# The last image of a convolution and attention kernel: x and the first two outputs summed in chunks during the last block, two rows completed by VectorE, two pairs in another buffer

## The chip, the cores and the metric

The kernel runs on one core of a Trainium2 chip. The metric is the device time of one execution in microseconds (us); lower is better. The profile is of one such execution; its times are counted from the start of its span, the stretch from the first to the last instruction.

## What is computed

x has 16 images of 128 channels and 64 x 64 points. Layer 0 normalizes each group of four channels of an image, rounds the result to 8 bits, adds a cubic term and convolves it 3 x 3 with three weight sets. The three outputs are each rounded and clipped, and summed with weights; the sum is scaled, biased and added to x. Layer 1 normalizes again, projects to q, k and v of 64 channels, mixes exp(k) and exp(k) v by exp(B), and adds the projected result.

```python
outs = [jnp.einsum('bctfyx,ocyx->btfo', fv, g[i]) for i in range(WP - 1)]
mem_out = adc(outs[-1])
for i, bit in enumerate(reversed(range(WP - 1))):
    mem_out = mem_out + adc(outs[i]) * 2.0 ** bit
mem_out = mem_out * output_factor
# layer 1, after  x = x + layer0(gn(x)):
num = jnp.einsum('ji,bit->bjt', eB, ek * v)
den = jnp.einsum('ji,bit->bjt', eB, ek)
out = q * (num / den)
out = jnp.einsum('oj,bjt->bot', Wm, out)
```

## The kernel before

The convolution is done in a transformed form (Winograd in both directions). Four rows of outputs come from six transformed row sets ("points"). A block is the work on one image and one weight set, so there are 48 blocks, in two halves each: half 0 with points 1 and 2, half 1 with points 3 and 4. Points 0 and 5 join at the end.

The program is one long list of named operations. A name such as `q31.5` is an operation, and the number after a plus sign says how many turns back its image lies. A turn holds the three blocks of one image, the input work of the next image and the second layer of the one or two before. The order of the list is the order in which each engine issues; an operation that has to wait holds up all that follow it on its engine. `ORDER` gives the steady turns, `FIRST` the first, and `LAST` the last: the rest of turn 14, turn 15 with the last image, and turn 16 with what is left. In `LAST`, +2 belongs to turn 14, +1 to turn 15, +0 to turn 16. The last image is image 15.

Names that matter, with k = 0 to 5 for the half that is being worked on:

- TensorE: `q1`, `q2`, `q0`, `q3` are the matmuls of a half with the points u = 0 and 1, into `pa` and `pb` (L556). `P.k` is the matmul that even and odd columns of an outer row share (`shared`), `o0.k` and `o1.k` the two outer matmuls of each column (`outer`), all into `py`. `kp`, `vp`, `qp` (L749) are projections of a pair, `dn` (L759) the mixing, `op` (L771) the output projection.
- ScalarE: `m1`, `sd`, `sA` copy `pa` (L579, L581, L584). `tk.k` (`take`, L633) reads the finished outer row from `py` as int16. `xn` (L796) normalizes the input of a pair, `ek`, `g`, `ln`, `ex`, `r` (L800, L775, L805, L806, L782) are steps of a pair. `cx` (`chunk`, L699) scales the summed outputs of a quarter of an image, `sq` and `ts` (L364) sum squares.
- VectorE: `Bo`, `df`, `sm` (L587, L588, L594) combine the points, `ma` and `mc` (`middle`, L610) make the two middle rows, `S0` and `S3` (`total`, L615 and L618) the sums that outer rows need, `bc` (`spread`, L625) adds these to the shared column in PSUM and spreads it over both columns, `bA`, `bB` (L636) clip, and `ekv`, `u`, `oa`, `ob`, `oc` (L801, L804, L807 to L809) are steps of a pair.
- GpSimd (POOL) issues transfers that add to their target: `sm.k` for even k (L596), `aA`, `aB` of the second and third weight set into `acc` (L643), `cdx` (x onto the scaled sum, L702) and `rd` (residual of a pair, L812). SP issues the plain ones: `li`, `lj` (loads of x), `st` (stores of a pair, L813).

An image is 4 pairs of 1024 points of each channel (`Pair`). In the steady turns a pair's normalized input, its result and the source of its store are one of two buffers, `xns[:, p % 2]`, so pair 2 of an image waits for the store of pair 0 of the same image, and pair 3 for that of pair 1.

The third block of image 15 is finished differently (`Last`, `End`, `LastPair`). Its names begin with t: `tma`, `tmc` make the middle rows, `tS0`, `tS1` the sums, `tP0`, `tP1` the shared matmuls, `tbc`, `tbd` the `spread`s, `tp0`, `tp1`, `to0`, `to1` the outer matmuls (the half h = 1 in `pb`, h = 0 in `py`), `tk0` and `tk3` the `take`s of rows 0 and 3, `tb0` to `tb3` the clipping. `ta0` to `ta3` add each clipped row to `acc` on VectorE (L684). Meanwhile SP has loaded x of image 15 into `x2e`, a view of `gmat`, in four chunks (`Lx0` to `Lx3`, L717). `tx0` to `tx3` (`part`, L724) then compute x + ofs * acc for a row and sum it, `ts0` to `ts3` sum its squares. After these come the norm (`tna` to `tnd`), and four pairs named with capitals (`Xn`, `Kp`, ...), each with buffers of its own.

Of the kernel before, what the change touches and what calls it, by code (L numbers as in the profile page):

```python
# [94 lines left out]
START = "x0 xa pmx xb pvx xc xl xd gr0 er0 cp gr1 er1 pb1 pa1 cs1 cq1 cd1"  # L95

LAST = """
    cl0+2 sA1.2+2 S3.2+2 q31.2+2 lj3+2 st2+2 q10.3+2 cl1+2 P.2+2 bc.2+2 m10.3+2 q11.3+2 m11.3+2
    s0+2 q20.3+2 q21.3+2 o0.2+2 Bo.2+2 va0+2 s1+2 va1+2 sd0.3+2 o1.2+2 bA.2+2 sd1.3+2 q01.3+2
    sq1+2 sq2+2 lj2+2 gr0+2 sq3+2 q30.3+2 q00.3+2 tk.2+2 sA1.3+2 er0+2 q31.3+2 sA0.3+2 ya+2  # L100
    df.2+2 n3+2 n2+2 pmy+2 yb+2 P.3+2 bc.3+2 Bo.3+2 cp+2 q11.4+2 pvy+2 q10.4+2 yc+2 cl3+2
    df.3+2 o0.3+2 m10.4+2 m11.4+2 o1.3+2 q20.4+2 q21.4+2 yl+2 s3+2 yd+2 xn0+2 sd0.4+2 sd1.4+2
    kp0+2 vp0+2 sm.3+2 tk.3+2 P.4+2 q01.4+2 cl2+2 sm.2+2 ek0+2 va3+2 mc.4+2 s2+2 st3+2 aA.2+2
    S0.4+2 ekv0+2 bc.4+2 dn0+2 sA1.4+2 g0+2 q00.4+2 sA0.4+2 va2+2 u0+2 xn1+2 ln0+2 o1.4+2 gr1+2
    o0.4+2 q30.4+2 oa0+2 ex0+2 kp1+2 er1+2 tk.4+2 qp0+2 ob0+2 vp1+2 q11.5+2 ma.4+2 oc0+2 S3.4+2
    ek1+2 m11.5+2 pb0+2 op0+2 r0+2 ekv1+2 q31.4+2 Bo.4+2 rd0+2 q10.5+2 pa0+2 m10.5+2 st0+2
# [12 lines left out]
    sm.1+1 q10.3+1 mc.2+1 S0.2+1 q31.2+1 cd3x+1 bc.2+1 e5+1 o0.2+1 ma.2+1 sq1+1 o1.2+1 S3.2+1
    sA1.2+1 Lx0+0 m10.3+1 tk.2+1 Bo.2+1 bA.2+1 q11.3+1 m11.3+1 q20.3+1 P.3+1 df.2+1 q21.3+1  # L120
    sd0.3+1 q00.3+1 bc.3+1 Lx1+0 o1.3+1 sq2+1 sd1.3+1 q30.3+1 st3+1 sq3+1 sA0.3+1 st2+1 ya+1
    pmy+1 yb+1 q31.3+1 pvy+1 yc+1 yl+1 Bo.3+1 q01.3+1 sA1.3+1 yd+1 sm.2+1 df.3+1 sm.3+1 q10.4+1
    m10.4+1 mc.4+1 o0.3+1 xn0+1 S0.4+1 q11.4+1 tk.3+1 kp0+1 vp0+1 P.4+1 ek0+1 ekv0+1 q20.4+1
    bc.4+1 xn1+1 dn0+1 g0+1 u0+1 sd0.4+1 o0.4+1 m11.4+1 oa0+1 ln0+1 o1.4+1 ex0+1 q21.4+1 ob0+1
    tk.4+1 kp1+1 ma.4+1 qp0+1 vp1+1 aA.2+1 oc0+1 S3.4+1 ek1+1 op0+1 ekv1+1 sd1.4+1 r0+1 q00.4+1
    q01.4+1 sA1.4+1 P.5+1 rd0+1 dn1+1 g1+1 bc.5+1 q11.5+1 bA.4+1 o1.5+1 st0+1 o0.5+1 sA0.4+1
    q30.4+1 u1+1 q10.5+1 aA.4+1 ln1+1 tk.5+1 oa1+1 ex1+1 xn2+0 qp1+1 ob1+1 q31.4+1 oc1+1 bB.3+1
    Bo.4+1 op1+1 kp2+0 r1+1 m10.5+1 vp2+0 aB.3+1 q20.5+1 df.4+1 ek2+0 m11.5+1 ekv2+0 sd0.5+1
    q21.5+1 sd1.5+1 dn2+0 q30.5+1 q01.5+1 g2+0 u2+0 ln2+0 oa2+0 rd1+1 q31.5+1 sA1.5+1 st1+1
    q00.5+1 qp2+0 bB.5+1 ex2+0 aB.5+1 Bo.5+1 xn3+0 sA0.5+1 kp3+0 vp3+0 ob2+0 oc2+0 op2+0 ek3+0  # L130
# [13 lines left out]
def conv_preact_kernel(  # L144
# [29 lines left out]
    P = 128  # L174
# [247 lines left out]
    class Input:  # L422
# [5 lines left out]
        def load(self, q):  # L428
            sp.dma_start(self.x[q], rows(x, self.b, q))
# [125 lines left out]
    def mm(o, w, r, start, stop):  # L555
        pe.matmul(  # L556
            o if len(r.shape) == 2 else o.rearrange("p (t w) -> p t w", w=W2), w, r,
            start=start, stop=stop, skip_group_check=True,
        )


    class Block:
# [35 lines left out]
        def part(self, h):  # L598

            a = acc[:, 1:3] if h == 0 else acc[:, 0:4:3]  # L600
            return (a if self.i == 0 else ys[h]), a
# [63 lines left out]
    class Last(Block):  # L665


        def value(self, r):
            return ys[r in (0, 3)][:, r // 2]

        def operations(self):
            o = {
                "tma": lambda: self.middle(0), "tmc": lambda: self.middle(1),
            }
            for h, z in ((0, py), (1, pb)):
                o |= {
                    f"tS{h}": lambda h=h: self.total(h), f"tP{h}": lambda h=h, z=z: self.shared(h, z),
                    f"tb{'cd'[h]}": lambda h=h, z=z: self.spread(h, z), f"tk{3 * h}": lambda h=h, z=z: self.take(h, z),
                }
                for c in range(2):  # L680
                    o[f"t{'op'[h]}{c}"] = lambda h=h, c=c, z=z: self.outer(h, c, z)
            for r in range(4):
                o[f"tb{r}"] = lambda r=r: self.bound(self.value(r))
                o[f"ta{r}"] = lambda r=r: dve.tensor_tensor(acc[:, r], acc[:, r], self.value(r), ALU.add)  # L684
            return o

    class End:
# [25 lines left out]
            return o  # L713


        def load(self, q):
            sp.dma_start(self.x2[q], rows(x, self.b, q))  # L717

        def row(self, r):
            return x2e.rearrange("p q (t r w) -> p r (q t) w", r=4, w=W)[:, r]  # L720

        def part(self, r, k):
            t = self.row(r)
            dve.scalar_tensor_tensor(  # L724
                t, acc[:, r], ofs, t, ALU.mult, ALU.add, accum_out=self.sums[:, 0, k : k + 1]
            )

        def part_square(self, r, k):
# [139 lines left out]
    def operations(c):  # L868

        o = {}  # L870
        for k in range(6):
            i, h = divmod(k, 2)
            if c < B:
                o |= blocks[c, i].half(h, k)
            if 0 < c < B or (c == 0 and i):
                o |= blocks[(c, i - 1) if i else (c - 1, 2)].rest(k)
        if c < B:
            o["p0"] = lambda: inputs[c].point(0, v[:, 0])
            o["e0"] = lambda: inputs[c].pairs(0)
            o["e5"] = lambda: inputs[c].pairs(1)  # L880
            o["p5"] = lambda: inputs[c].point(5, v[:, 1])
        if 0 < c < B:
            ends[c - 1] = End(c - 1, inputs[c - 1].norm.mean, x2s)
            o |= ends[c - 1].operations()
            for p in (0, 1):
                o |= Pair(ends[c - 1], p).operations()
        if 1 < c:
            for p in (2, 3):
                o |= Pair(ends[c - 2], p).operations()
        if c + 1 < B:  # L890
            inputs[c + 1] = Input(c + 1)
            o |= inputs[c + 1].operations()
        return o
# [64 lines left out]
```

## Time and profile before

| | us |
|---|---|
| three runs | 1597.41, 1597.85, 1602.0; median 1597.85 |
| profiled execution, its own time | 1598.49 |
| its span | 1596.8 |
| busy: TensorE, VectorE, ScalarE, GpSimd | 1487.7, 1479.8, 1183.0, 224.0 |
| mean granted TensorE clock | 0.981 |
| last outer matmul of the convolution ends | 1553.99 |
| last `part` (tx3) ends | 1559.05 |

A steady turn takes about 94 us. Busy times count the engine's own instructions; a wait belongs to the engine that stands still. A line with "<-" after a time names what ended an engine's wait. Records of a matmul with 512 columns come in twos.

### The profile page before, as it was taken

The page shows a single profiled execution, that of the slowest core. Times are in us where ns is not written, and L with a number is a line of the kernel's source. Part 1 is how long each engine was busy: PE and PEld are TensorE (multiplying, and loading weights), DVE is VectorE, ACT ScalarE, POOL GpSimd, SP SyncE. Part 2 cuts the span into 40 slices and gives each one's busy share as a digit, 9 for nine tenths or more (in the row PEclk, how much of TensorE's full clock was granted, in tenths as well). Part 3 has the DMA queues.
Part 4 walks back from the last instruction along what each step waited for, and adds up shares of the span by engine and source line. Part 5 has one row for each costly group of instructions (what it writes and reads, how often), then busy time and mean ns, then how long its engine had stood idle before and what let it go on. Part 6 is the DMA issues. An engine that isn't in the chain of part 4 may idle for free.

```text
span 1596.8 us, 14936 instructions
## 1 busy us (share of the span) xinstructions
PE 1487.7 (93%) x4680; PEld 563.4 (35%) x4680; DVE 1479.8 (93%) x1919; ACT 1183.0 (74%) x1857; POOL 224.0 (14%) x250
## 2 busy tenths in 40 slices
PE   1798999999999999999999999999999999999985
PEld 0233433333333333333333343333333333333321
DVE  7999999999999999999999999999999999998775
ACT  7656878787777878778787877878778787766655
POOL 2001011121201112020111201111120111202010
PEclk6899999999999999999999999999999999999998
DMA  6235467594746758465684746659474675836462
GB/s 186 79 92 120 103 160 171 126 204 114 148 128 164 184 119 196 120 137 141 150 205 109 156 131 150 166 132 203 117 152 132 156 176 121 196 66 119 119 158 80
DMA packets 67361, 227.03 MB, mean 142 GB/s; under 512 B 7632, under 2 KB 8272, under 8 KB 67280
## 3 DMA queue, kind: packets, MB, share of 16 engines
q0 software_dynamic: 37904, 123.42, 42.1%
q1 hardware_dynamic: 29088, 101.59, 17.9%
q10 hardware_dynamic: 288, 1.05, 0.2%
q8 instruction: 37, 0.61, 0.2%
q14 instruction: 44, 0.36, 0.1%
HBM read 102.30 MB, written 33.55 MB: 85 GB/s over the span
## 4 chain that ended last, share of the span: by engine, by line
PE 58%; DMA 14%; issue 11%; DVE 11%; ACT 5%; POOL 2%; DVEq 0%; POOLq 0%; ACTq 0%; SPq 0%
PE py L556 19%; PE pa L556 18%; DMA x<-in_x_dram 5%; PE pz L749 5%; PE pb L556 5%; PE pz L759 3%; PE py L749 3%; DMA s<-s 3%; DMA acc<-y 3%; PE py L771 3%; ACT x L699 2%; DVE acc L610 1%; ACT gs L364 1%; DVE y L610 1%; DVE s L615 1%
## 5 line engine op out<-in xcount | busy, mean ns | idle before, releaser
L556 PE MATMUL py<-v,ud 128*128 128x512 f32 x760 | 357.0, 608 | 1.9 <-DVE py L625 1.3
L556 PE MATMUL pa<-cs,us 128*128 128x512 f32 x384 | 199.1, 620 | 41.7 <-DVE cs L514 31.9
L556 PE MATMUL pa<-cd,us 128*128 128x512 f32 x384 | 203.9, 622 | 11.7 <-ACT pb L581 11.7
L556 PE MATMUL pa<-cq,us 128*128 128x512 f32 x384 | 198.1, 612 | 11.3 <-ACT d L579 11.2
L556 PEld LDWEIGHTS py<-v,ud 128*128 128x128 f32 x760 | 138.9, 189 | 184.0 <-issue 148.9
L556 PE MATMUL pb<-cd,us 128*128 128x512 f32 x384 | 194.5, 602 | 1.9 <-ACT pb L581 1.7
L579 ACT ACTIVATE d<-pa 128x512 f32<-128x512 f32 x192 | 112.2, 594 | 37.8 <-PE pa L556 28.0
L812 POOL DMA_DIRECT2D xn<-x x60 | 59.9, 998 | 567.8 <-ACT xn L782 567.5
L581 ACT ACTIVATE pb<-pa 128x512 f32<-128x512 f32 x192 | 112.5, 586 | 31.3 <-PE pa L556 30.7
L584 ACT ACTIVATE s<-pa 128x512 f32<-128x512 f32 x192 | 110.4, 591 | 32.0 <-PE pa L556 29.9
L749 PE MATMUL pz<-xn,w 128*64 128x512 f32 x480 | 121.8, 607 | 1.3 <-ACT xn L796 1.2
L587 DVE SCALAR_TENSOR_TENSOR s<-d,pb 128x1024 f32<-128x1024 f32 x96 | 117.2, 1221 | 3.6 <-PE pb L556 3.2
L643 POOL DMA_DIRECT2D acc<-y x62 | 68.5, 1105 | 360.8 <-DVE y L636 212.2
L588 DVE TENSOR_TENSOR d<-s 128x1024 f32<-128x1024 f32 x96 | 117.5, 1224 | 1.6 <-ACT s L584 1.5
L633 ACT ACTIVATE y<-py 128x1024 int16<-128x1024 f32 x63 | 84.0, 1334 | 46.0 <-PE py L556 44.8
L782 ACT ACTIVATE xn<-py,scalars 128x512 f32<-128x512 f32 x120 | 76.0, 685 | 56.1 <-PE py L771 56.0
L556 PEld LDWEIGHTS pa<-cs,us 128*128 128x128 f32 x384 | 66.3, 191 | 139.6 <-issue 67.0
L556 PEld LDWEIGHTS pa<-cq,us 128*128 128x128 f32 x384 | 68.0, 190 | 119.5 <-issue 69.4
L556 PEld LDWEIGHTS pa<-cd,us 128*128 128x128 f32 x384 | 66.4, 190 | 123.6 <-ACT pb L581 56.9
L556 PEld LDWEIGHTS pb<-cd,us 128*128 128x128 f32 x384 | 70.2, 190 | 96.0 <-issue 85.2
L556 PE MATMUL py<-sv,ud 128*128 128x512 f32 x190 | 97.7, 596 | 3.3 <-ACT y L633 3.2
L596 POOL DMA_DIRECT2D s<-s x48 | 45.9, 956 | 339.5 <-DVE d L588 127.9
(224 smaller groups left out, 2651.8 us busy)
## 6 DMA issues: line engine op xcount, KB each, us to landing
xc<-in_x_dram SPq DMA_DIRECT2D x121, 512.0 KB, 5.6
acc<-y POOLq DMA_DIRECT2D x62, 512.0 KB, 5.5
x<-in_x_dram POOLq DMA_DIRECT2D x60, 512.0 KB, 10.4
xn<-x POOLq DMA_DIRECT2D x60, 512.0 KB, 4.9
out_dram<-xn SPq DMA_DIRECT2D x60, 512.0 KB, 5.1
s<-s POOLq DMA_DIRECT2D x48, 512.0 KB, 6.3
gmat<-in_x_dram SPq DMA_DIRECT2D x5, 512.0 KB, 8.9
x<-in_g_neg_dram SPq DMA_DIRECT2D x2, 576.0 KB, 11.4
```

The source lines that it names most:

```text
L556: pe.matmul(o if len(r.shape) == 2 else o.rearrange("p (t w) -> p t w", w=W2), w, r, start=start, stop=stop, skip_group_check=True,)
L579: f"m1{u}.{k}": lambda u=u, a=a: act.activation(d[:, u], a, AF.Copy),
L581: f"sd{u}.{k}": lambda a=a, b=b: act.activation(b, a, AF.Copy, scale=-1.0),
L584: f"sA{u}.{k}": lambda u=u, a=a: act.activation(s[:, u, 0], a, AF.Copy),
L587: f"Bo.{k}": lambda: dve.scalar_tensor_tensor(s[:, :, 1], d, 2.0, pb, ALU.mult, ALU.add),
L588: f"df.{k}": lambda: dve.tensor_tensor(d, s[:, 1], s[:, 0], ALU.subtract),
L633: act.activation(self.column(self.part(1)[0], h), y, AF.Copy)
L643: pool.dma_start(a, y, accum_op=ALU.add)
L749: pe.matmul(self.tiles(o)[h * IC : (h + 1) * IC], w, x[:, t[0] : t[1] : t[2]], start=True, stop=True)
L759: pe.matmul(o[c, t], eb[r, c], self.half(x)[r, t], start=True, stop=True, skip_group_check=True)
L782: act.activation(g[:, t], self.tiles(self.op[h]), AF.Identity, bias=bias_sb)
L812: "rd": lambda: pool.dma_start(self.r, self.x2, accum_op=ALU.add),
```

## The change

In the third block of image 15:

- The sum of the first two weight sets' outputs, which is complete in `acc` once `aA.4+1` and `aB.5+1` have landed, is scaled into `x2e` by ScalarE in four chunks (`Lc0` to `Lc3`, `early`). x is then added by four accumulating transfers of POOL (`Lx0` to `Lx3`, `input`) instead of being loaded by SP. `part` adds ofs times the clipped row of the third weight set to that; `ta0` to `ta3` are dropped.
- `shared` is issued for both columns, so the two `spread`s (`tbc`, `tbd`) are dropped. `tk0` and `tk3` are now `complete` on VectorE: PSUM plus the sum of the other points, as int16. The half h = 1 goes to `pz` instead of `pb`.
- In turn 16, pairs 2 and 3 of image 14 have their normalized input, result and source of the store in `f` instead of `xns`.
- `LAST` is written anew throughout. `rd0+1`, `rd1+1`, `st0+1`, `st1+1` (the residuals and stores of pairs 0 and 1 of image 14) now stand after the norm of image 15; `Lx0` and `Lx1` stand in turn 16's part instead of turn 15's; `tk.5+2`, `ln1+2`, `ex1+2` precede `xn2+1`, and `sA1.1+1` precedes `cx0+1`.

```diff
@@ LAST, the part from the end of the last image's convolution to its norm
-    q00.5+1 qp2+0 bB.5+1 ex2+0 aB.5+1 Bo.5+1 xn3+0 sA0.5+1 kp3+0 vp3+0 ob2+0 oc2+0 op2+0 ek3+0
-    r2+0 df.5+1 tma+0 ekv3+0 sm.5+1 tS1+0 dn3+0 g3+0 u3+0 ln3+0 tP1+0 tbd+0 ex3+0 qp3+0 sm.4+1
-    oa3+0 ob3+0 oc3+0 tp0+0 op3+0 tmc+0 tS0+0 tb2+0 tp1+0 Lx2+0 Lx3+0 r3+0 tP0+0 tb1+0 ta1+0
-    tbc+0 to1+0 tx1+0 ta2+0 tk3+0 tx2+0 tb3+0 tsh+0 to0+0 ta3+0 tk0+0 tb0+0 ts1+0 ta0+0 ts2+0
-    tx0+0 ts0+0 tx3+0 ts3+0 tna+0 tpm+0 rd2+0 tnb+0 tpv+0 tnc+0 tnl+0 tnd+0 Xn0+0 Xn2+0 Xn1+0
+    g1+1 u1+1 ln1+1 o0.5+1 q30.4+1 oa1+1 tk.5+1 ex1+1 m10.5+1 bB.5+1 xn3+0 aB.5+1 kp2+0 qp1+1
+    ob1+1 oc1+1 sA1.4+1 vp2+0 op1+1 ek2+0 ekv2+0 q11.5+1 r1+1 dn2+0 g2+0 oa2+0 m11.5+1 u2+0
+    Lc0+0 Lx0+0 q20.5+1 ln2+0 ex2+0 q31.4+1 Bo.4+1 sd0.5+1 q21.5+1 ob2+0 kp3+0 qp2+0 oc2+0
+    vp3+0 Lc1+0 op2+0 sd1.5+1 q01.5+1 ek3+0 ekv3+0 dn3+0 df.4+1 q30.5+1 Lc2+0 sA1.5+1 g3+0
+    q31.5+1 Lx2+0 q00.5+1 r2+0 u3+0 ln3+0 oa3+0 Bo.5+1 ex3+0 ob3+0 qp3+0 sA0.5+1 df.5+1 sm.4+1
+    tP1+0 tp0+0 Lx1+0 oc3+0 sm.5+1 tma+0 op3+0 Lc3+0 Lx3+0 r3+0 tmc+0 tb1+0 tp1+0 tP0+0 tS1+0
+    tb2+0 tS0+0 rd3+0 tx1+0 tk3+0 tsh+0 ts1+0 to0+0 tx2+0 ts2+0 to1+0 tk0+0 tb3+0 tb0+0 tx0+0
+    ts0+0 tx3+0 ts3+0 st3+0 tna+0 tpm+0 tnb+0 tpv+0 tnc+0 tnl+0 tnd+0 Xn0+0 Xn2+0 Xn1+0 Kp0+0
+    rd1+1 Vp0+0 Ek0+0 rd0+1 Eq0+0 Kp1+0 Dn0+0 Ek1+0 Gg0+0 Uu0+0 Xn3+0 st1+1 Vp1+0 Oa0+0 Kp2+0
...
-        def shared(self, h, y):
-            mm(y[:, 1], ud[self.i][:, h, 0], sv[:, h], True, True)
+        def shared(self, h, y, c=1):
+            mm(y[:, c], ud[self.i][:, h, 0], sv[:, h], True, True)
...
+        def complete(self, h, y):
+            t = self.d[0] if h else ss[1][:, 1]
+            dve.tensor_tensor(self.column(self.part(1)[0], h), y, t, ALU.add)
+
         def value(self, r):
             return ys[r in (0, 3)][:, r // 2]
...
-            for h, z in ((0, py), (1, pb)):
+
+            for h, z in ((0, py), (1, pz)):
                 o |= {
-                    f"tS{h}": lambda h=h: self.total(h), f"tP{h}": lambda h=h, z=z: self.shared(h, z),
-                    f"tb{'cd'[h]}": lambda h=h, z=z: self.spread(h, z), f"tk{3 * h}": lambda h=h, z=z: self.take(h, z),
+                    f"tS{h}": lambda h=h: self.total(h),
+                    f"tP{h}": lambda h=h, z=z: [self.shared(h, z, c) for c in range(2)],
+                    f"tk{3 * h}": lambda h=h, z=z: self.complete(h, z),
                 }
...
-                o[f"ta{r}"] = lambda r=r: dve.tensor_tensor(acc[:, r], acc[:, r], self.value(r), ALU.add)
...
-        def load(self, q):
-            sp.dma_start(self.x2[q], rows(x, self.b, q))
+        def early(self, q):
+            a = acc[:, :, 4 * q : 4 * q + 4].rearrange("p r t w -> p t r w")
+            act.activation(self.x2[q].rearrange("p (t r w) -> p t r w", t=4, r=4), a, AF.Copy, scale=ofs)
...
-        def part(self, r, k):
+        def part(self, r, k, a):
             t = self.row(r)
             dve.scalar_tensor_tensor(
-                t, acc[:, r], ofs, t, ALU.mult, ALU.add, accum_out=self.sums[:, 0, k : k + 1]
+                t, a, ofs, t, ALU.mult, ALU.add, accum_out=self.sums[:, 0, k : k + 1]
             )
...
-                o |= Pair(ends[c - 2], p).operations()
+                pair = Pair(ends[c - 2], p)
+                if c == B:
+
+                    pair.xn = f.rearrange("p r w -> p (r w)")[:, bass.ts(p - 2, CH)]
+                    pair.r = pair.xn
+                o |= pair.operations()
...
-    turns[B] = operations(B) | Last(B - 1, 2).operations()
+    last = Last(B - 1, 2)
+    turns[B] = operations(B) | last.operations()
     end = End(B - 1, None, x2e, banks=(pa[0], pa[0]))
     for q in range(NCH):
-        turns[B][f"Lx{q}"] = lambda q=q: end.load(q)
+        turns[B][f"Lc{q}"] = lambda q=q: end.early(q)
+        turns[B][f"Lx{q}"] = lambda q=q: end.input(q)
     for k, r in enumerate((1, 2, 0, 3)):
-        turns[B][f"tx{r}"] = lambda r=r, k=k: end.part(r, k)
+        turns[B][f"tx{r}"] = lambda r=r, k=k: end.part(r, k, last.value(r))
```

`input`, which the change calls, stood there before: `pool.dma_start(self.x2[q], rows(x, self.b, q), accum_op=ALU.add)`.

## The prediction

> **What bounds the kernel now.** I read the busy table and its sums by stage first. The stages are one steady stretch, the stretches of the rewritten order (it begins near 1384 us), and the tail. Columns: stage, us, busy PE, PEld, DVE, ACT, POOL with counts, granted clock, DMA share, GB/s.
>
> ```profile
> PE 1487.7 (93%) x4680; PEld 563.4 (35%) x4680; DVE 1479.8 (93%) x1919; ACT 1183.0 (74%) x1857; POOL 224.0 (14%) x250
> ...
> 1200.00:1300.00 100.00, 97.86 (x307) 37.37 (x306) 96.44 (x122) 78.50 (x123) 14.80 (x16) 1.00 0.67 159
> 1384.00:1420.00 36.00, 33.45 (x102) 13.05 (x102) 34.15 (x47) 26.93 (x39) 0.85 (x1) 1.00 0.39 105
> 1420.00:1460.00 40.00, 38.64 (x142) 14.22 (x141) 37.56 (x39) 21.04 (x32) 6.34 (x7) 1.00 0.51 109
> 1460.00:1500.00 40.00, 38.52 (x97) 15.12 (x97) 31.51 (x43) 27.61 (x46) 7.18 (x8) 1.00 0.76 168
> 1500.00:1554.00 54.00, 49.52 (x187) 16.97 (x185) 39.34 (x52) 27.45 (x40) 6.34 (x7) 1.00 0.50 115
> 1554.00:1597.00 43.00, 23.64 (x132) 7.62 (x132) 22.01 (x44) 23.18 (x35) 1.69 (x2) 0.82 0.30 89
> ```
>
> TensorE bounds the body: 2 us idle in a steady 100. Up to 1460 VectorE is nearly as full (94 to 95%), afterwards it has room. Between 1384 and 1554 TensorE loses about 10 us; that is all an order can win there. After 1554 comes a serial tail. Next, who made TensorE wait (total us, times, longest):
>
> ```profile
> PE pa L556 <- ACT s L584: 1.8, 2, 1.1
> PE pz L383 <- DVE y L378: 1.8, 2, 1.4
> PE py L556 <- DVE py L625: 1.3, 1, 1.3
> PE py L749 <- ACT y L633: 1.3, 1, 1.3
> PE pz L749 <- ACT xn L796: 1.2, 1, 1.2
> PE pz L759 <- DVE ekv L801: 0.9, 1, 0.9
> PE pb L556 <- DVE pb L625: 0.9, 1, 0.9
> ```
>
> Last the timeline around the end of the convolution, and the two rows of the page on the accumulating transfers:
>
> ```profile
> 1550.21 3.78 PE L556 MATMUL py<-v,ud 128*128 128x512 f32 x8 [1.33 <-DVE py L625]
> ...
> 1554.03 1.30 ACT L633 ACTIVATE y<-py 128x1024 int16<-128x1024 f32 x1 [4.65 <-PE py L556]
> ...
> 1555.82 0.69 DVE L684 TENSOR_TENSOR acc<-acc,y 128x1024 int16<-128x1024 int16 x1
> ...
> 1556.55 1.28 DVE L724 SCALAR_TENSOR_TENSOR gmat<-acc,scalars,gmat 128x1024 f32<-128x1024 int16 x1
> ```
> ```profile
> x<-in_x_dram POOLq DMA_DIRECT2D x60, 512.0 KB, 10.4
> ...
> s<-s POOLq DMA_DIRECT2D x48, 512.0 KB, 6.3
> ```
>
> The last `part` (tx3) ends at 1559.05; from there squares, norm and four last pairs run one behind the other to 1596.8, 37.75 us.
>
> **TensorE in the last block.** `shared` now writes both columns, so one more matmul in each of tP1 and tP0: a matmul is two records at 0.43 us (x8 took 3.78 with four matmuls), so 2 x 0.86 = +1.72. Removed are four waits of the second table. The third pair's `xn3` stood behind the store of `xns` (1.21 at 1534.91, and 0.86 at 1538.76 which follows from it); it now writes into `f`, whose last reader is cd1+2, at 1461 to 1463. The two `spread`s stood between shared and outer matmuls (0.85 at 1542.77, 1.33 at 1550.21); they are gone, and what waits for VectorE is `complete`, after the matmuls. Sum -4.25. The new order changes between kinds of matmul (convolution, projection, mix, output) 54 times instead of 58; after a change the timeline shows 1.01 to 1.06 for what takes 0.86 otherwise, so 4 x 0.17 = -0.6. The last outer matmul, 1553.99 before, ends at 1553.99 - 4.25 + 1.72 - 0.6 = 1550.9, if all before starts as before.
>
> **The stretch ahead (L).** Three waits there have a named cause that the new order moves. 1.30 at 1435.52: tk.5+2 stood on ScalarE behind xn2+1, which waited 5.15 us for the store of pair 0. Now ln1, ex1, sA0.5 and tk.5 precede it, and between op0+2 and kp2+1 lie some 14 us of matmuls, against r0 1.3 + rd0 5.1 + store 4.6 + xn2 1.24 = 12.2. 1.07 at 1472.58: sA1.1+1 stood behind two `chunk`s that wait for the acc transfer; now it precedes them. 0.41 at 1491.54: the mean of image 14 waits for x landing at 1489.25, 12.6 us after issue, in a burst of eight transfers. Two of these (Lx0, Lx1 by SP) leave the burst. L = 2.78. The 1.41 at 1396.50 stays: its x was issued ahead of the rewrite. Bounds for L: none of it and two new waits of 1.2 (bB.3+2, aB.3+2, 1.36 us of VectorE work, move forward into a stretch where VectorE has 1.9 of 36 us free), or all of it and half of the 1.41; -2.4 to +3.5.
>
> **VectorE decides the end.** Let T be the end of q31.5+1. Behind it TensorE has q00.5 0.86, qp3 0.96, tP1 1.82, tp0 1.72, op3 1.06, tp1 1.82, tP0 1.82, to0 1.72, to1 1.72: 13.5. So T = 1550.9 - 13.5 = 1537.4, less L. VectorE, in order, begins Bo.5 at T: 1.17, ob3 0.65, df.5 1.2, oc3 0.65, sm.5 1.15, tma 1.35, tmc 1.35, tb1 0.38, tS1 1.2, tb2 0.38, tS0 1.2, tx1 1.2, tk3 1.3, tsh 0.12, tx2 1.25, tk0 1.3, tb3 and tb0 0.8, tx0 1.2, tx3 1.36: 19.2. Four `ta` (0.69, L684) and two `spread`s (1.23, L625) have gone, 5.2 us; two `complete`s came. No row has PSUM and SBUF in, int16 out: below it is 1.23 (L625, two such sources), above 1.37 (L610, int16 with stride); 1.3. [...] TensorE is done at T + 13.5, tk0 begins at T + 14.5: VectorE is the later one. tx3 ends at 1537.4 + 19.2 - L = 1556.6 - L, 2.45 + L = 5.2 sooner.
>
> **ScalarE and the queues.** Four `early` (Lc) come: L699's 1.13 without its accumulator, 4 x 1.13 = 4.5; two `take`s of 1.3 go. ScalarE is at half load there (27.45 of 54), so this costs nothing while each Lc meets ready data. Lc0 waits for the landing of aB.5: tk.5 ends near T - 15.7, bB.5 at T - 14.9, plus 5 is T - 9.9; ScalarE reaches Lc0 at T - 9.7. Queued behind it are ln2, ex2, sd0.5, Lc1, sd1.5, ek3; TensorE needs sd1.5 by T - 3.7 and has it at T - 4.8. Without that cover a late Lc0 costs its lateness less 1.1. The four Lx leave SP (they waited there for nothing) for POOL, between aB.5 and sm.4: Lx0, Lx2 (Lc2 done at T - 3.0), sm.4 (df.4 at T - 2.3), Lx1, Lx3 (Lc3 at T + 2.75), each 0.85 of issue. tmc needs sm.4 at T + 6.2; tx1 needs Lx3 at T + 10.7. A lone transfer here takes 4.5, x at least 6.6 and in a burst up to 15.2. [...] Lx3 at 2.8 + 7.8 = T + 10.6, just in time. rd1, rd0, st1, st0 of image 14 go behind Lx3 and into the tail, four transfers of 2.2 to 5.7 us; DMA is 30% busy there, nothing waits for them but the end, some 25 us later. SP loses its four loads. The tail swaps Kp2 and Qp0 and small neighbours: nothing either way, -0.5 to +0.5. [...]
>
> **Sum.** The profiled execution took 1598.49 for its span of 1596.8. Gain 2.45 + 2.78 = 5.23: span 1591.6, time 1593.3. Against the median 1597.85, 0.64 lower, that is 1592.6, 0.33% faster.
>
> **Rivals.** (a) The gain ahead is hidden or refilled: VectorE is as full as TensorE up to 1460 and new waits eat L. Then 1597.85 - 2.45 = 1595.4. For it: the first three stage rows; against: causes are named for each wait. (b) Slower: the one POOL queue is late. acc, Lx0, Lx2, sm.4, Lx1, Lx3 form a dependent row there. If aB.5 takes 8.2 as at 1532.03, Lc0 is 3.3 late and 2.2 to 3 reach T; if Lx3 takes 15.1 as at 1379.14, tx1 is 7.3 late: 10.3 together, 1602.9. It decides once the lateness passes 5.2. For it: the median of x is 10.4, which alone makes 2.5; against: those were bursts with SP's transfers beside them, and SP has none here but one store. (c) The waits that xn3 left return elsewhere on ScalarE: 1594 to 1595, counted with (a).
>
> **How the numbers follow.** A measurement of this kernel can tell about 0.3% (4.8 us) from no change. Main case 0.58, own range 1589 to 1595 (0.50 of it beyond 0.3%); (a) with (c) 0.18, mostly within (0.04 faster, 0.12 same, 0.02 slower); (b) 0.24, of it 0.17 beyond 0.3% slower and 0.07 within. Faster 0.54, same 0.27, slower 0.19. The range is 1589 to 1602.5: main and (a) whole, (b) up to nearly its point.
>
> **What the profile after would show.** No wait of TensorE for L625 near the end; no xn waiting for out_dram; tx3's end 5 us earlier; tk0 of VectorE directly behind tx2. Wrong would be: tx1 or tmc waiting for a POOL transfer, ScalarE idle before an Lc, a tail longer than 38 us, or new waits of TensorE between 1384 and 1500.

## The result, and the profile after

The changed kernel took 1596.45 us (median of 12 runs, 1593.51 to 1599.81). The kernel before, run beside it, took 1602.18 (median of 12, 1596.13 to 1606.15). The ratio of the runs is 0.997, 95% interval 0.9957 to 0.9984. A second batch gave 1595.81 against 1599.42, ratio 0.9973 (0.9961 to 0.9986). The forecast was 1592.6 and 0.33% faster: its sign and share hold, its time is 3.9 us too low. The two numbers come apart because the kernel before, 1597.85 in three runs, has a median of 1599.0 to 1602.2 in larger batches. That turned out to have a cause of its own, found below.

The profiled execution took 1596.26 for a span of 1594.6, against 1598.49 and 1596.8: only 2.2 us. Busy table and sums by stage of the changed kernel, columns as before:

```profile
PE 1488.2 (93%) x4684; PEld 564.8 (35%) x4684; DVE 1476.9 (93%) x1915; ACT 1184.6 (74%) x1859; POOL 227.8 (14%) x254
...
1384.00:1420.00 36.00, 34.50 (x103) 13.25 (x104) 34.37 (x48) 26.68 (x39) 0.86 (x1) 1.00 0.38 103
1420.00:1460.00 40.00, 39.38 (x145) 15.28 (x144) 38.94 (x41) 21.98 (x34) 7.21 (x8) 1.00 0.51 109
1460.00:1500.00 40.00, 36.57 (x90) 14.45 (x88) 28.53 (x39) 25.84 (x42) 6.33 (x7) 0.96 0.69 142
1500.00:1554.00 54.00, 51.22 (x196) 18.56 (x192) 38.28 (x49) 32.46 (x47) 10.05 (x11) 1.00 0.51 92
1554.00:1597.00 43.00, 23.42 (x132) 7.53 (x132) 21.31 (x44) 19.85 (x32) 1.69 (x2) 0.75 0.48 142
```

The first two stages and the fourth gained TensorE work (33.45 to 34.50, 38.64 to 39.38, 49.52 to 51.22; in the fourth, 1.72 are the added matmuls). The third lost it: 36.57 instead of 38.52, and its granted clock fell from 1.00 to 0.96. The waits of TensorE from 1384 to 1560 name the place (total us, times, longest):

```profile
PE pa L384 <- DVE y L379: 8.5, 1, 8.5
PE pa L557 <- ACT d L580: 3.4, 1, 3.4
PE py L557 <- ACT acc L634: 0.8, 1, 0.8
PE pa L557 <- ACT s L585: 0.8, 1, 0.8
PE pz L756 <- ACT xn L803: 0.6, 1, 0.6
```

The first row is the norm, the beginning of the tail. Of the rows of before, the two `spread` rows and the waits of the third pair (`xn`, `ekv`) are gone, as forecast. The 1.41 us at 1396.50 for the mean of image 13 is gone too, which the forecast had left standing; 0.83 us for `tk.2` (L634) came in its place at 1395.81. The large new one is 3.4 us for L580, the copy `m1` of `pa`. The timeline of the changed kernel around it (start, duration, engine, line, in brackets the idle time and what ended it):

```profile
1458.10 0.84 POOL L597 DMA_DIRECT2D s<-s  x1 [3.16 <-DVE d L589]
1458.70 1.12 POOL L644 DMA_DIRECT2D acc<-y  x1
1463.22 1.19 POOL L644 DMA_DIRECT2D acc<-y  x1 [3.40 <-DVE y L637]
...
1470.77 1.15 ACT L705 ACTIVATE x<-acc,scalars 128x1024 f32<-128x1024 int16 x1 [2.42 <-DMA acc<-y]
...
1474.69 0.58 ACT L580 ACTIVATE d<-pa 128x512 f32<-128x512 f32 x1
...
1475.32 1.68 PE L557 MATMUL pa<-cq,us 128*128 128x512 f32 x2 [3.43 <-ACT d L580]
...
1476.79 1.91 PE L557 MATMUL pa<-cd,us 128*128 128x512 f32 x2
```

The same stretch of the kernel before:

```profile
1455.84 1.20 POOL L643 DMA_DIRECT2D acc<-y  x1
1460.60 0.85 POOL L596 DMA_DIRECT2D s<-s  x1 [3.56 <-DVE d L588]
1464.60 1.19 POOL L643 DMA_DIRECT2D acc<-y  x1 [3.15 <-DVE y L636]
...
1469.67 1.15 ACT L699 ACTIVATE x<-acc,scalars 128x1024 f32<-128x1024 int16 x1 [0.48 <-DMA acc<-y]
...
1472.58 1.12 PE L556 MATMUL pa<-cs,us 128*128 128x512 f32 x2 [1.07 <-ACT s L584]
```

The chunks `cx` scale the summed outputs of image 14 and cannot begin before the transfer `aB.1` (the last of the three rows of POOL in each) has landed. Before, it landed 4.99 us after its issue and ScalarE waited 0.48. After, it landed 7.46 us after, although it was issued 1.4 us sooner, and ScalarE waited 2.42 in front of `cx0`. `m11.2` stands behind three chunks on ScalarE, and TensorE waits for `m11.2`. What had changed ahead of `aB.1` is the place of `aA.0`. Before, it left at 1455.84 and had landed by 1462.4. After, it left at 1458.70, right behind `sm.0`, took 8.45 us and landed at 1467.15, so it was still under way for 3.9 us after `aB.1` had joined it. A store of SP at 1458.96 is new there as well; the experiment with `aA.0` below keeps that store. After the wait come matmul pairs of 1.91 us where 1.02 is usual.

The end of the convolution in the changed kernel, VectorE's timeline:

```profile
1537.53 1.22 DVE L588 SCALAR_TENSOR_TENSOR s<-d,pb 128x1024 f32<-128x1024 f32 x1
...
1543.61 1.36 DVE L611 SCALAR_TENSOR_TENSOR y<-s,s 128x1024 int16<-128x1024 f32 x1
...
1549.21 1.29 DVE L731 SCALAR_TENSOR_TENSOR gmat<-y,scalars,gmat 128x1024 f32<-128x1024 int16 x1 [1.32 <-DMA gmat<-in_x_dram]
1550.42 1.29 DVE L671 TENSOR_TENSOR y<-pz,d 128x1024 int16<-128x1024 f32 x1
...
1552.86 1.30 DVE L671 TENSOR_TENSOR y<-py,s 128x1024 int16<-128x1024 f32 x1
...
1556.04 1.28 DVE L731 SCALAR_TENSOR_TENSOR gmat<-y,scalars,gmat 128x1024 f32<-128x1024 int16 x1
```

`Bo.5` begins at 1537.53, tx3 ends at 1557.33 (with the read of its sum). `tmc` at 1543.61 finds its transfer `sm.4` just landed, at 1543.52. `tx1` at 1549.21 waits 1.32 us for `Lx3`.

The two stretches can be told apart at `dn0+1`, the mixing of pair 0 of image 14: at its end both kernels have done the same work. In us, from the two traces:

| | before | after | difference | forecast |
|---|---|---|---|---|
| `dn0+1` ends | 1502.24 | 1503.39 | +1.15 | -2.78 |
| from there to the last outer matmul | 51.75 | 47.83 | -3.92 | -3.13 |
| from there to the end of tx3 | 56.80 | 53.94 | -2.86 | -2.45 |
| from tx3 to the end | 37.74 | 37.23 | -0.51 | 0 |

So the end of the convolution gave what was forecast and more, and the stretch ahead of it gave nothing: it lost 1.15 us where 2.78 were to be won. From 1384 to the end of `dn0+1` TensorE stands still for 5.38 us before and 5.54 after: the waits removed were made up by the new one, and the half clock came on top.

### The profile page after: what moved, and what is told of

It reads as the page before. It is cut to its first block, busy times and chain, and to the rows that moved or that the text cites. A ratio compares the mean times of both kernels' runs of the same rounds, so it can differ in the third digit from the quotient of the medians.

```text
span 1594.6 us, 14947 instructions
## 1 busy us (share of the span) xinstructions
PE 1488.2 (93%) x4684; PEld 564.8 (35%) x4684; DVE 1476.9 (93%) x1915; ACT 1184.6 (74%) x1859; POOL 227.8 (14%) x254
## 4 chain that ended last, share of the span: by engine, by line
PE 54%; issue 14%; DMA 13%; DVE 12%; ACT 5%; POOL 2%; DVEq 0%; POOLq 0%; ACTq 0%; SPq 0%
PE py L557 18%; PE pa L557 17%; PE pz L756 5%; PE pb L557 5%; DMA x<-in_x_dram 4%; PE pz L766 3%; DMA s<-s 3%; PE py L756 3%; DMA acc<-y 3%; PE py L778 2%; ACT x L705 2%; DVE acc L611 1%; DMA gmat<-in_x_dram 1%; DVE y L611 1%; DVE s L616 1%
## 5 line engine op out<-in xcount | busy, mean ns | idle before, releaser
L580 ACT ACTIVATE d<-pa 128x512 f32<-128x512 f32 x192 | 112.1, 594 | 36.3 <-PE pa L557 20.4
L756 PE MATMUL pz<-xn,w 128*64 128x512 f32 x464 | 117.7, 607 | 0.6 <-ACT xn L803 0.6
L634 ACT ACTIVATE y<-py 128x1024 int16<-128x1024 f32 x62 | 82.6, 1333 | 41.4 <-PE py L557 40.2
```

The costliest lines, as they stand in the source:

```text
L580: f"m1{u}.{k}": lambda u=u, a=a: act.activation(d[:, u], a, AF.Copy),
L634: act.activation(self.column(self.part(1)[0], h), y, AF.Copy)
L756: pe.matmul(self.tiles(o)[h * IC : (h + 1) * IC], w, x[:, t[0] : t[1] : t[2]], start=True, stop=True)
```

## The experiments

In the expectations, theory A is the account just given (the parts at the end work as forecast, what is lost is lost on the way there), theory B the rival of each run; in the runs on the spread of the kernel before, theory A is that a wait behind a transfer differs from one execution to the next. L numbers in kernels whose list was wrapped anew lie 2 to 4 lower than above.

### The parts of the change, one at a time on the kernel before

**The other buffer alone.**

```diff
-                o |= Pair(ends[c - 2], p).operations()
+                pair = Pair(ends[c - 2], p)
+                if c == B:
+                    pair.xn = f.rearrange("p r w -> p (r w)")[:, bass.ts(p - 2, CH)]
+                    pair.r = pair.xn
+                o |= pair.operations()
```

> The kernel before with one part alone: pairs 2 and 3 of image 14 in f, the old order kept. Theory A (the end of the change is a chain on VectorE behind q31.5, and what this buffer frees is one wait of 1.21 and one of 0.86 of TensorE behind xn3): xn3 no longer waits for a store, TensorE's last outer matmul ends 1 to 2 us earlier, tx3 1 to 2 us earlier, ratio to before 0.999. Theory B (the buffer is the whole of the change): about 5 us, ratio 0.997. Theory C (another wait takes the place of the store): no difference, ratio 1.000.

Measured: 1597.75 against 1599.12, ratio 0.9987 (0.9975 to 0.9998). The wait for `xn` at 1534.91 has gone, the one for `ekv` behind it stays as 1.1 (0.86 before), the two `spread` waits are there. From `dn0+1` to tx3 it takes 55.65, 1.15 less than before, close to the wait at its row, 1.21. So the 0.86, which the forecast took to follow from the wait for `xn3`, does not go with the buffer; it went with the order.

**`complete` and the double `shared` alone.**

```diff
+        def complete(self, h, y):
+            t = self.d[0] if h else ss[1][:, 1]
+            dve.tensor_tensor(self.column(self.part(1)[0], h), y, t, ALU.add)
...
-f"tk{3 * h}": lambda h=h, z=z: self.take(h, z),
+f"tk{3 * h}": lambda h=h, z=z: self.complete(h, z),
...
-tP1+0 tbd+0 ex3+0
+tP1+0 ex3+0
...
-ta1+0 tbc+0 to1+0
+ta1+0 to1+0
```

> The kernel before with one part alone: shared for both columns, no spread, rows 0 and 3 completed by VectorE; the old order less the two spreads. Theory A: TensorE's waits of 0.85 and 1.33 for L625 go, two matmuls (1.72) come; on VectorE two of 1.23 go and two of 1.3 come; tx3 0 to 1 us earlier, ratio 0.9995 to 1.000. Theory B: it is this part that brings the gain, 2.5 us or more, ratio 0.998. Theory C: the PSUM read on VectorE costs, tx3 1 us or more later, ratio 1.001.

Measured: 1598.77, ratio 0.9996 (0.9984 to 1.0008), no difference. From `dn0+1` to tx3 it takes 56.45, 0.35 less. Without the order and the other parts, the 2.2 us of waits saved and the 1.72 us of added matmuls nearly cancel.

**x and the first outputs summed in chunks, alone, in the old order.** The four `Lc` and the four `Lx` stand behind `sm.4+1`, and the four `ta` are dropped.

```diff
-sm.4+1 oa3+0
+sm.4+1 Lc0+0 Lx0+0 Lc1+0 Lx1+0 Lc2+0 Lx2+0 Lc3+0 Lx3+0 oa3+0
```

> The kernel before with one part alone: the chunks (Lc on ScalarE, Lx by POOL, no ta), each right behind sm.4 in the old order, where aB.5 lands at 1540.2 only. Theory A (the part needs its new place: acc complete 13 us earlier): Lc0 waits for acc until about 1543, the four Lx land at 1555 to 1560, tx1 (1550.07 before) waits for them, tx3 5 to 9 us later, ratio 1.003 to 1.006. Theory B (transfers are hidden anyway, VectorE saves four of 0.69): 1 to 3 us sooner, ratio 0.999.

Measured: 1603.79, ratio 1.0033 (1.0022 to 1.0044): slower. VectorE's timeline in this kernel:

```profile
1558.30 1.28 DVE L722 SCALAR_TENSOR_TENSOR gmat<-y,scalars,gmat 128x1024 f32<-128x1024 int16 x1 [7.35 <-DMA gmat<-in_x_dram]
```

Here `acc` is complete only late, and the four x transfers of POOL leave together from 1544.54 to 1548.24; the last takes 9.9 us and makes `tx1` wait 7.35. That the slower rival of the forecast had 7.3 for such a wait is chance: it had the transfer take 15.1 us, and here a late issue does most of it. The place of the chunks and transfers in the new order is what keeps this away in the changed kernel.

### Where the gain ahead went

**The changed kernel once more**, for a second trace of the 3.43.

> The changed kernel once more, for a second trace and beside the others on one chip. Theory A (the 3.43 us of TensorE at 1475.32 are the order's own: m11.2 stands behind three chunks, and these behind acc's landing): the wait is there again, 2.5 to 4 us, tx1 waits again 0.5 to 2 us for x; ratio 0.9965 to 0.9985. Theory B (chance of the transfers in one execution): the wait is 1 us or less, and the tail begins 2 us or more earlier.

Measured: 1595.81, ratio 0.9973 (0.9961 to 0.9986). TensorE waits 3.39 at 1474.95 for L580, tx1 waits 1.33 for its x. The wait is the order's doing and is in both traces.

**`m11.2` and what hangs on it ahead of the chunks.** In this kernel `sd0.2` and `sd1.2` overwrite `pb` before `Bo.1` has read it, so the part of the outputs that `Bo.1` makes is not the reference's; the amount of work is the same.

```diff
-q11.2+1 cx1+1 cx2+1
+q11.2+1 P.2+1 m11.2+1 sd0.2+1 cx1+1 q21.2+1 sd1.2+1 cx2+1
```

> The changed kernel with one more move: in turn 15, m11.2, sd0.2 and sd1.2 stand ahead of the later chunks (cx1, cx2), so TensorE's 3.43 us at 1475.32 does not wait for three chunks behind the landing of acc. Theory A (the stretch ahead gave its gain back at this wait, and the half clock of 3.4 us after it comes from it): that wait falls to 1 us or less and the clock stays at 1.0 there; the norm of image 14, which hangs on the same transfers, then makes TensorE wait 1 to 3 us at its mean; 1 to 3.5 us faster than the changed kernel, ratio to before 0.995 to 0.9965. Theory B (the transfers set the pace from there on): the same time as the changed kernel, ratio 0.997, the wait found again whole at the mean. Theory C: the end is set by the POOL queue alone, tx1 waits as much longer as TensorE is earlier.

Measured: 1597.99, ratio 0.9989 (0.9979 to 0.9999). The wait for L580 has gone, but the next copy behind a chunk takes its place:

```profile
1480.48 1.13 PE L554 MATMUL pa<-cs,us 128*128 128x512 f32 x2 [3.14 <-ACT s L582]
```

1 to 3.5 us were expected; the median is 1.5 to 2.2 us above those of the changed kernel. Moving the instruction that TensorE waits for past the chunks does not remove the wait; the chunks are late, and someone stands behind them. The profiled execution, 1595.19, is the fastest of the twelve, so the trace does not show where the median lost.

**The order around the join turned so that chunks come between shorter pieces of work.**

```diff
-q11.2+1 cx1+1 cx2+1 p5+1
+q11.2+1 P.2+1 p5+1
...
-Bo.1+1 sd0.2+1 P.2+1 df.1+1
+Bo.1+1 m11.2+1 sd0.2+1 cx1+1 q21.2+1 q00.2+1 sd1.2+1 q30.2+1 sA0.2+1 cx2+1 df.1+1
...
-cd2x+1 cx3+1
+cd2x+1 q01.2+1 sA1.2+1 cx3+1
...
-m10.4+1 yc+1 q01.3+1 yl+1 yd+1 sA1.3+1 o1.3+1
+m10.4+1 q01.3+1 ya+1 pmy+1 yb+1 sA1.3+1 o1.3+1 pvy+1 yc+1 yl+1 yd+1
```

> The changed kernel with the join loosened: on ScalarE m11.2, sd0.2, sd1.2 and sA0.2 stand ahead of the chunks cx1 and cx2 or cx3 they stood behind, with Bo.1 ahead of sd0.2; and the mean and variance matmuls of image 14's norm stand 5 matmuls later on TensorE. Theory A (the stretch ahead gave 2 to 3 us back at that wait): the wait falls below 1 us, no wait above 1.5 us comes at the norm, the last outer matmul ends 2 to 3 us earlier, tx1 waits no longer than 2 us more for x; ratio 0.9955 to 0.997, 1 to 3 us faster than the changed kernel in the same call. Theory B (the transfers of acc and x set the pace whatever the order): the sum of the waits stays, same time as the changed kernel.

Measured: 1601.66, ratio 1.0008 (0.9996 to 1.0021): the changed kernel's gain is lost. Theory A failed here, which had 1 to 3 us for this order. TensorE's timeline, and one line of VectorE's:

```profile
1478.99 1.36 DVE L608 SCALAR_TENSOR_TENSOR acc<-s,s 128x1024 int16<-128x1024 f32 x1 [4.92 <-ACT x L702]
...
1483.99 2.80 PE L554 MATMUL py<-v,ud 128*128 128x512 f32 x4 [4.13 <-DVE py L623]
1486.59 1.91 PE L554 MATMUL pa<-cq,us 128*128 128x512 f32 x2
```

`bc.2` on VectorE (L623) stands behind `mc.2`, which writes into `acc` (L608) and must wait until the chunks have read it. With the chunks later, VectorE is what is late. Neither of the two reorderings reached the cause, which lies ahead of the chunks.

**`aA.0` sooner.** `bA.0` and `aA.0` go right behind `tk.0`, so that `aA.0` has landed before `sm.0` and `aB.1` are issued. Nothing else is touched.

```diff
-tk.0+1 q30.0+1
+tk.0+1 bA.0+1 aA.0+1 q30.0+1
...
-df.0+1 bA.0+1 g3+1
+df.0+1 g3+1
...
-ex3+1 aA.0+1 sd0.1+1
+ex3+1 sd0.1+1
```

> The changed kernel with one clipping and its transfer moved: bA.0 and aA.0 of the block before stand behind tk.0, about 7 us earlier, so the transfer aB.1 that the chunks wait for has no other close ahead of it in POOL's queue. Theory A (the 3.4 us of TensorE at 1475 come from acc landing late, 7.5 us after issue): aB.1 lands about 5 us after issue, the wait falls to 0.5 to 1.8 us, the clock stays at 1.0 there, tx3 2 to 4 us earlier; ratio 0.995 to 0.9965. Theory B (the pace is set elsewhere, or the move costs as much on VectorE, which is full there): ratio as the changed kernel's, 0.997.

Measured: 1593.05 (1592.65 to 1595.3), ratio 0.9958 (0.9943 to 0.9974): 3.4 and 2.8 us below the two medians of the changed kernel, and the best of all. The two kernels were not run side by side, and the intervals of their ratios overlap; but five of these six runs took at most 1593.82, and of the changed kernel's twenty only one did. The timeline of this kernel:

```profile
1450.54 0.85 POOL L641 DMA_DIRECT2D acc<-y  x1 [11.31 <-DVE y L634]
...
1457.64 0.85 POOL L594 DMA_DIRECT2D s<-s  x1 [3.17 <-DVE d L586]
1462.75 1.19 POOL L641 DMA_DIRECT2D acc<-y  x1 [4.27 <-DVE y L634]
...
1467.83 1.15 ACT L702 ACTIVATE x<-acc,scalars 128x1024 f32<-128x1024 int16 x1
...
1472.39 1.12 PE L554 MATMUL pa<-cq,us 128*128 128x512 f32 x2 [0.96 <-ACT d L577]
...
1473.35 1.02 PE L554 MATMUL pa<-cd,us 128*128 128x512 f32 x2
```

`aA.0` leaves at 1450.54 and has landed by 1455.02. `aB.1` lands 4.99 us after its issue instead of 7.46, `cx0` begins without a wait, TensorE waits 0.96 instead of 3.43, and the pairs after it take 1.02. The sums from 1470 to 1480, first of the changed kernel, then of this one, show the clock:

```profile
1470.00:1480.00 10.00, 6.57 (x12) 2.56 (x11) 6.86 (x8) 6.81 (x12) 3.40 (x4) 0.83 0.86 182
```
```profile
1470.00:1480.00 10.00, 9.04 (x21) 3.44 (x20) 9.11 (x11) 6.73 (x14) 2.77 (x4) 1.00 1.00 200
```

0.83 over 10 us is 3.4 us at half clock: in the changed kernel the granted clock is 0.50 in each us from 1476 to 1479. From the start of the pair that waited to that of the third pair behind it, the changed kernel takes from 1475.32 to 1479.70 and this one from 1472.39 to 1475.15, so half clock costs 1.6 us. With the wait's 2.5 that is 4.1, against 3.7 us between the two spans; a wait of 0.75 at 1481.49 comes back here.

**The two moves alone**, in the old order: `xn2+1` behind `tk.5+2`, the chunks behind `sA1.1+1` and `m10.2`.

```diff
-bB.3+2 xn2+1 bA.4+2
+bB.3+2 bA.4+2
...
+tk.5+2 xn2+1 sA1.5+2
...
-q30.1+1 cx1+1 p0+1
+q30.1+1 p0+1
...
-q01.1+1 cx0+1 sA1.1+1
+q01.1+1 sA1.1+1
...
+m10.2+1 cx1+1 cx0+1 df.1+1
```

> The kernel before with two moves of order alone, those of which the prediction took 1.30 and 1.07: xn2+1 stands behind ln1, ex1 and tk.5 of turn 14, and sA1.1 and m10.2 stand ahead of the chunks. Theory A (what is won ahead is given back where m11.2 waits for chunks behind acc's landing): the wait of 1.30 falls below 0.8, a wait of 1.5 to 3 us appears at the matmul behind m11.2, ratio 0.9995 to 1.000. Theory B (the prediction's L): both waits go, 2 to 2.5 us, ratio 0.9985.

Measured: 1605.37, ratio 1.0037 (1.0026 to 1.0049): slower. TensorE's waits in this kernel:

```profile
PE pa L554 <- ACT s L582: 3.9, 1, 3.9
PE pz L747 <- ACT xn L794: 3.9, 2, 2.6
PE pa L554 <- ACT d L577: 2.2, 2, 1.9
```

Neither theory had this kernel slower. The two waits that the forecast counted as removed (1.30 and 1.07) come back larger behind the next instructions: 2.6 for `xn` itself, 1.9 and 3.9 for copies behind the chunks. The two moves are worth nothing by themselves.

### The buffer and the queue at the end

**The changed kernel without the other buffer.** Pairs 2 and 3 of image 14 use `xns` again, so the residuals and stores of pairs 0 and 1 must stand ahead of `xn2+0` and `xn3+0`.

```diff
-                if c == B:
-                    pair.xn = f.rearrange("p r w -> p (r w)")[:, bass.ts(p - 2, CH)]
-                    pair.r = pair.xn
...
-op0+1 r0+1 q21.4+1
+op0+1 r0+1 rd0+1 st0+1 xn2+0 q21.4+1
...
-r1+1 dn2+0
+r1+1 rd1+1 st1+1 xn3+0 dn2+0
```

> The changed kernel with the buffer undone: pairs 2 and 3 of image 14 in xns again, so xn2 and xn3 wait for the stores of pairs 0 and 1, whose residuals and stores stand right behind r0 and r1 again. Theory A (the new order needs the buffer: xn3 cannot start before op1 + r1 1.3 + residual 4.6 + store 3.5): xn2 makes TensorE wait 1.5 to 3 us, xn3 holds ScalarE about 8 us ahead of g2 and Lc0, and the end moves 5 to 9 us later than in the changed kernel; ratio 1.000 to 1.003. Theory B (the buffer is worth what it is worth in the old order, 1 to 2 us): ratio 0.998 to 0.999.

Measured: 1620.33, ratio 1.0123 (1.0105 to 1.0141), 24.5 above the changed kernel, where 5 to 9 were expected. The mechanism is the expected one, its size was far underestimated. TensorE's timeline:

```profile
1525.83 2.07 PE L554 MATMUL pa<-cd,us 128*128 128x512 f32 x2 [11.14 <-ACT pb L579]
...
1549.81 2.07 PE L554 MATMUL pa<-cq,us 128*128 128x512 f32 x2 [7.27 <-ACT d L577]
```

ScalarE stood 10.3 and 7.6 us in front of the two `xn`, and everything behind them on ScalarE with it, the copies of the convolution too. The new order needs the buffer.

**`Lx1` ahead of `Lx2` and `sm.4`**, to bring `Lx3` forward.

```diff
-Lc1+0 op2+0
+Lc1+0 Lx1+0 op2+0
...
-tp0+0 Lx1+0 oc3+0
+tp0+0 oc3+0
```

> The changed kernel with Lx1 issued right behind Lc1, ahead of Lx2 and sm.4 in POOL's order. Theory A (tx1's wait of 1.3 us is the queue's: Lx3 lands 8.4 us after issue because Lx1 was issued only 4 us before it): Lx3 lands 6 to 7.5 us after issue, tx1 waits 0 to 0.5 us, tmc none, tx3 0.8 to 1.3 us earlier; ratio about 0.9965. Theory B (sm.4 is pushed back by it): tmc waits 1 us or more, no gain.

Measured: 1596.77, ratio 0.9978 (0.9967 to 0.999), the same as the changed kernel. VectorE's timeline:

```profile
1545.19 1.35 DVE L608 SCALAR_TENSOR_TENSOR y<-d,d 128x1024 int16<-128x1024 f32 x1
1548.76 1.33 DVE L608 SCALAR_TENSOR_TENSOR y<-s,s 128x1024 int16<-128x1024 f32 x1 [2.22 <-DMA s<-s]
```

`Lx3` now lands 7.63 us after its issue and `tx1` waits for nothing, but `sm.4` has two x transfers close ahead, lands 10.08 us after its issue and holds `tmc` for 2.22. Theory B was right: the queue hands the lateness on.

### Why the kernel before spreads

**The kernel before once more**, one execution.

> The kernel before once more, for a second trace of it. Theory A (its waits behind a landing transfer are marginal and differ from one execution to the next): the wait near 1434 behind xn2+1 or that near 1472 differs by 1 us or more from 1.30 and 1.07, or the clock halves somewhere between 1384 and 1554; time 1596 to 1604. Theory B (the first trace is typical): the same waits within 0.2 us and no half clock there.

Measured: 1603.85, span 1602.1. The mixing of the pairs, from first to last, in the first execution of the kernel before and in this one (the two times at the end of a row are the first and last start):

```profile
L759 PE MATMUL pz<-ek,eb x32: 376/402/427, 1501.2 to 1539.1; 64*64 64x256 f32 x32
```
```profile
L759 PE MATMUL pz<-ek,eb x32: 376/402/427, 1506.4 to 1544.4; 64*64 64x256 f32 x32
```

All 5.3 us of difference lie ahead of 1501. The sums from 1430 to 1450 of the two executions, and the wait in the second:

```profile
1430.00:1450.00 20.00, 18.64 (x63) 6.70 (x62) 18.12 (x19) 11.96 (x18) 2.03 (x2) 1.00 0.53 119
```
```profile
1430.00:1450.00 20.00, 16.84 (x52) 5.24 (x50) 14.09 (x15) 8.06 (x12) 1.07 (x2) 0.83 0.32 75
...
1435.78 1.24 ACT L796 ACTIVATE xn<-x,y 128x1024 f32<-128x1024 f32 x1 [7.85 <-DMA out_dram<-xn]
...
1437.08 1.98 PE L749 MATMUL pz<-xn,w 128*64 128x512 f32 x4 [2.76 <-ACT xn L796]
```

`xn2+1` waits for the store of pair 0 of image 14, which took 6.07 us here and 4.60 in the first execution. TensorE waits 2.76 + 0.40 instead of 1.30, 1.9 us more, and 6.83 us at half clock follow (0.83 over 20 us). Not all of the 5.3 comes from this: the second execution is 1.25 us behind at 1396 already (1397.75 against 1396.50 at the same matmul). At the first mixing matmul after the wait it is 5.95 behind (1449.18 against 1443.23). So the long form costs 4.7 us, 1.9 for the wait and 2.8 for the half clock, and 0.7 of it is made up again by 1501. To test this, one last kernel takes the wait away, by giving pairs 2 and 3 of image 13 buffers whose last readers are done near 1390:

```diff
-                o |= Pair(ends[c - 2], p).operations()
+                pair = Pair(ends[c - 2], p)
+                if c == B - 1:
+                    pair.xn = pair.r = xc[p - 2]
+                o |= pair.operations()
```

> The kernel before, with one thing changed: pairs 2 and 3 of image 13 (xn2+1, xn3+1 and their r, rd, st in turn 15) use xc[0] and xc[1], whose last readers are the n2+2 and n3+2 near 1390, in place of xns. So xn2+1 no longer waits for the store of pair 0 of image 14. Theory A: the executions of the kernel before spread over 8 us (1596 to 1604 in most calls) because that wait near 1434 ends either soon (TensorE waits 1.3 us) or late (2.6 to 2.8 us and a half clock of 6.83 us after it, as in the repeated look at the kernel before). Then this kernel shows no wait for xn or for the take behind it near 1434, no half clock there, its executions keep within 5 us, few or none above 1600, and the median falls by 1.5 to 3.5 us. Theory B: the spread comes from elsewhere (the burst of transfers near 1480, or ahead of the rewritten order). Then the median falls by at most 1.3 us, and executions still reach 1602 to 1604 with a spread of 7 us or more.

Measured: 1597.23 (1595.99 to 1599.86, 12 runs) against 1600.06 (1596.43 to 1604.78, 17 runs), ratio 0.9985 (0.9973 to 0.9997). Its spread is 3.9 us instead of 8.4, and none of its runs passes 1600, where 9 of 17 of the kernel before did. Its row for 1430 to 1450:

```profile
1430.00:1450.00 20.00, 20.00 (x68) 7.06 (x66) 19.42 (x20) 11.03 (x16) 2.03 (x2) 1.00 0.54 121
```

TensorE is never idle there. Theory A holds: more than half of the spread of the kernel before is this one wait. Where the remaining 3.9 us come from is not shown.

## Why the prediction was right or wrong

**TensorE in the last block: right.** The waits for `xn3` and the two `spread`s are gone, and from `dn0+1` to the last outer matmul the changed kernel is 3.92 us shorter where 3.13 was worked out. 0.8 more came; the traces do not say from where. That the wait for `ekv` goes with the one for `xn3` was not so with the buffer alone.

**The stretch ahead, L = 2.78: the step that failed.** The forecast took 1.30, 1.07 and 0.41 as removed because the new order takes away what stood ahead of the waiting instruction. 1.30 became 0.62 and 0.41 vanished, but 1.07 became 3.43, and the half clock after it cost 1.6 more. The 1.41 that was to stay went as well, for 0.83 in its place; without that unforeseen gain the stretch would have lost more. What makes up the rest between these sums and the 1.15 is not shown. The range of L, -2.4 to +3.5, holds the measured -1.15, and rival (a), the gain refilled, gave 1595.4, within 1.1 of the measured median; but its reason, VectorE being full, was not the one. The chunks themselves were late, because one transfer was issued 2.9 us later and thereby got in the way of another. The forecast followed the instructions on their engines through the rewritten list and did this for POOL's queue only near the end. Moving `aA.0` back shows what the step was worth: that kernel's last outer matmul ends at 1548.11 and its tx3 at 1553.76, where the forecast, with L, had 1548.1 and 1553.8. That both agree so closely is in part luck: in that kernel `dn0+1` ends 1.96 us sooner than before instead of 2.78, and from there to the last outer matmul 3.92 are won instead of 3.13. Two of the forecast's own signs of being wrong came: `tx1` waits for a POOL transfer, and TensorE has new waits between 1384 and 1500; tx3 ends 1.7 us earlier, not 5.

**VectorE decides the end: right, with one wait more.** From `Bo.5` to tx3 19.8 us, of which 1.32 is the wait of tx1; without it 18.5, forecast 19.2. `complete` took 1.29 and 1.30, as the rows on both sides of it said (1.3).

**ScalarE and the queues: right to about 1 us.** `Lc0` waited for nothing (`aB.5` landed at 1527.57, ScalarE came at 1528.03). `sm.4` landed 7.84 us after its issue, taken as 7.7, which the s transfer issued at 1372.42 took in the kernel before, 0.57 us behind another of POOL; so it was 0.1 us in time. It landed 3.1 us after `Lx2`, which was issued 1.3 us ahead of it. The mis-sized term is `Lx3`: 8.39 us from issue to landing, taken as 7.8; with an issue 0.25 later and VectorE 0.35 sooner than worked out this makes most of the 1.32. Rival (b) named the place, and had it decide at 5.2 us of lateness; it came to 1.3.

**The tail: right.** 37.23 and 37.59 in two executions of the changed kernel, against 37.74.

**The sum against the median: right by two errors.** Profile against profile the change won 2.2 us and not 5.2. Median against median it won 5.7 and 3.6. Part of the difference is most likely that the new order also does away with the long form of the wait for `xn2+1`: TensorE waits 0.62 at 1434.70 in one execution and not at all in the other, with no half clock there. The forecast had priced that wait at the 1.30 of the one execution that it read, and set its sum against a median of three. The long form costs 4.7 us more at its place, and taking this wait away alone moved the median by 2.8. So the share of 0.33% was met by luck: too much was expected of the stretch ahead, and too little of that wait. By the medians the change won 0.36 and 0.23%, by the ratios 0.30 and 0.27%; the intervals take in both sides of the 0.3% that the forecast set as its bound.

## What to carry to other kernels

When an order is rewritten, follow each transfer through its queue as closely as each instruction through its engine: a transfer with no reader for 10 us may still delay the next one that has a reader (`aB.1` behind `aA.0`: 7.46 us instead of 4.99), and moving it forward (here `aA.0`, 2.8 to 3.4 us in the medians, against 3.6 to 5.7 for the whole change) can be worth nearly as much as the rest of the work. When a wait is removed, ask what is late behind it; here the waiting instruction could be moved past the chunks without gain, because the chunks were what was late. And before pricing a wait from one trace, look at the spread of the runs: a wait that ends just after a transfer lands can be twice as long in the next execution (here 1.30 in one, 2.76 + 0.40 in the other).

## What the runs showed that was not expected

A wait of TensorE in the middle of the body was not always paid once. After the 3.43 of the changed kernel came 3.41 us at half clock (granted clock 0.50); after the 2.76 in the second execution of the kernel before came 6.83, and after the 2.6 of the kernel with `complete` alone the same (0.83 from 1430 to 1450 in both). After the 11.14 and the 7.27 without the buffer came pairs of 2.07, and the mean granted clock of that execution was 0.975, against 0.980 of the changed kernel. Where it was worked out, somewhat less than half of that was added to the wait: 1.6 of 3.41 and 2.8 of 6.83. After the 3.14 of the kernel with `m11.2` ahead (pairs of 1.13 and 1.02 behind it) and the 2.6 of the two moves alone (1.00 from 1430 to 1450) there was none. So the length of the wait alone does not decide it; what does was not tried.

Accumulating transfers of POOL took much longer than 4.5 us when another was still under way. Of 512 KB each, `aA.0` took 4.48 with nothing close ahead (at 1450.54) and 8.45 with `sm.0` issued 0.6 us ahead; `aB.1` took 7.46 when `aA.0` was to land 3.9 us after its issue, but 4.99 when `sm.0` was to land 0.7 us after it; an s transfer behind two of x took 10.08. One that is issued sooner into a busy queue can land later: `aB.1` left at 1463.22 and landed at 1470.68 in the changed kernel, against 1464.60 and 1469.59 in the kernel before.
